# Ranks within experts: differences of router values as TensorE products, signs on VectorE and ScalarE in turn

## The chip, the cores and the metric

The kernel runs on one core of a Trainium2 chip. The metric is device time in microseconds (us) of one launch, the median of three runs. The core's engines work side by side, each through its own instructions in order: PE (TensorE, matrix products into PSUM), DVE (VectorE), ACT (ScalarE) and POOL (GpSimd); SP issues most transfers. PEld in the profile is PE's loading of stationary operands, which runs beside its products.

## What is computed

The reference is a network of four layers on 2048 tokens of 256 channels. Only the last step of the last layer is touched: a mixture of 16 experts in which each token goes to the expert with the highest router probability, and each expert takes at most 160 tokens, those with the highest probability.

```python
cap = math.ceil(CAP_FACTOR * bt / n)            # 1.25 * 2048 / 16 = 160
probs = jax.nn.softmax(jnp.einsum('btd,dn->btn', x, Wg), axis=-1)
top1_val, top1_idx = probs.max(-1).reshape(bt), probs.argmax(-1).reshape(bt)
masked = jnp.where(top1_idx[None, :] == jnp.arange(n)[:, None], top1_val[None, :], -jnp.inf)
vals, idx = jax.lax.top_k(masked, cap)          # per expert, best first
xe = x_flat[idx]
h = jax.nn.gelu(jnp.einsum('ncd,ndh->nch', xe, W1) + b1[:, None, :])
out = jnp.einsum('nch,nhd->ncd', h, W2) + b2[:, None, :]
y_flat = x_flat.at[safe_idx.reshape(-1)].set(out.reshape(-1, d), mode='drop')
```

So every token needs its rank among the tokens of its own expert: how many of them have a higher value, or the same value and a lower index. Tokens with ranks below 160 are gathered, go through two products and are written back.

## The kernel before

Tokens lie in 16 tiles of 128; four tiles make a chunk of 512. The class `Last` (from L1678) computes the ranks. Per chunk q it has three preparing steps and then one comparison ("unit") for each tile t up to the chunk's last one: 4, 8, 12 and 16 units for the four chunks, 40 in all.

- `logits` (L1739) makes the router's logits by PE, `top` (L1751) finds each token's best expert and its value by DVE, with one Exp on ACT.
- `rows` (L1771, called by `last`) turns values and experts, which lie one token per partition, into rows that lie along the free dimension and are the same on all partitions. PE transposes a broadcast (L1781), and ACT copies the result into the two halves `vb` and `eb` of `HT` (L1783). It also counts, by a product with ones (L1785), the tokens of the same expert in earlier tiles.
- `beats(t)` (L1797) compares the 128 tokens of tile t, on the partitions, with up to 512 tokens of chunk q, along the free dimension. ACT squares the difference of the experts (`l3f_dq`, L1802): zero for the same expert, at least 16 otherwise. DVE asks in one instruction whether the other value is higher and whether that 1 or 0 exceeds the square (`l3f_b`, L1822); its accumulator gives the sum along the row. PE sums the columns, 128 of them per product, against a single column of ones (`l3f_cs`, L1829), and DVE copies these sums into `acc` (L1836). Where the tile lies in the chunk itself, its own 128 x 128 square is compared apart, with ties, by three DVE instructions (`l3f_tie`, L1813, L1816, L1817).

`finish` (L1852) sends these steps out by hand: the rest of the previous mixture's additions (`c.pair`, three pairs of tiles: loads `yt<-tbuf`, DVE additions L1315, PE transposes L1241, ACT copies L1244) alternates with the steps of the four chunks. The steps of chunk 0 up to `last` are called earlier, from the loop over the shared expert (L1206). Then DVE sums `acc` into ranks (`l3f_rank`, L1875), compares them with the places 0 to 159 (`l3f_A`, L1879), PE turns that into row numbers (`l3f_pi`, L1884), and `run` (L1914) gathers rows by POOL and computes 20 slots of tokens, with results written by POOL (L1933).

Two facts of scheduling matter. Each engine takes its instructions in one fixed order, which is planned when the program is built, out of the order in which the code names them and the data they need; the planner may pull an instruction ahead of one that still waits. And tiles of PSUM are taken from pools: the tag "mm" has four buffers of one bank, "o" and "t" have two each.

Of the kernel before, what the change touches and what calls it, by code (L numbers as in the profile page):

```python
# [8 lines left out]
F32 = mybir.dt.float32  # L9
# [77 lines left out]
def _consts(k):  # L87
# [9 lines left out]
    k.after = cp.tile([P, P], F32, name="after")  # L97
    nc.gpsimd.affine_select(out=k.after, in_=k.ones, compare_op=ALU.is_ge, fill=0.0,
                            base=-1, pattern=[[-1, P]], channel_multiplier=1)
# [18 lines left out]
    k.one16 = cp.tile([P, 1], BF16, name="one16")  # L118
    nc.vector.memset(k.one16, 1.0)

# [1557 lines left out]
class Last:  # L1678

    E, F = 16, 512

    def __init__(self, k):
        self.k, E = k, self.E
        rp = k.rp
        self.w = []
        self.parts = [self.chunk(q) for q in range(NB)]

        self.plan = {5: [0], 6: [0], 7: [0]}  # L1690
        self.oh = rp.tile([P, NT, E], F32, name="l3f_oh")
        self.val = rp.tile([P, NT], F32, name="l3f_val")
        self.neg = rp.tile([P, NT], F32, name="l3f_neg")
        self.cum = rp.tile([P, NT + 1, E], F32, name="l3f_cum")

        self.acc = rp.tile([P, NT, 10], F32, name="l3f_acc")

        self.ids = rp.tile([P, NT, 2, E], BF16, name="l3f_ids")
        self.down = rp.tile([P, E], F32, name="l3f_down")
        self.th = rp.tile([P, NT], F32, name="l3f_th")  # L1700

        self.vb, self.eb = k.HT[:, 0, :], k.HT[:, 1, :]
        self.outs = []
# [11 lines left out]
    def begin(self):  # L1715

        k, nc = self.k, self.k.nc
        nc.vector.memset(self.acc, 0.0)
        nc.vector.memset(self.cum[:, 0, :], 0.0)
        nc.vector.tensor_scalar(self.down, k.iota[:, 0:self.E], -1.0, float(self.E), ALU.mult, ALU.add)  # L1720
        nc.vector.tensor_scalar_add(self.th, k.iota[:, 0:NT], 1.0)
        nc.sync.dma_start(k.hx[:, D:2 * D].rearrange("(t p) d -> p t d", p=P), k.Xt)
        self.weights()

# [4 lines left out]
    def chunk(self, q):  # L1729
# [41 lines left out]
        def rows(mul, mm):  # L1771
            nc.vector.tensor_scalar_mul(self.neg[:, ts], got["f"], -4.0)
            oh = self.oh[:, ts, :]
            nc.vector.tensor_tensor(oh, _bc(self.down, 1, [P, 4, E]), _bc(got["f"], 2, [P, 4, E]),
                                    ALU.is_equal)
            for t in range(4 * q, 4 * q + 4):
                nc.vector.tensor_add(self.cum[:, t + 1, :], self.cum[:, t, :], self.oh[:, t, :])
            for src, dst in ((got["f"], self.eb), (self.val[:, ts], self.vb)):
                ps = psum.tile([P, 4, P], F32, name="l3f_rb", tag="mm")
                for j in range(4):  # L1780
                    i = nc.tensor.transpose(ps[:, j, :], src[:, j:j + 1].to_broadcast([P, P]), k.ident)  # L1781
                    behind(i, mm)
                nc.scalar.copy(dst[:, cols], ps.rearrange("p j q -> p (j q)"))  # L1783
            ps = psum.tile([P, 4, E], F32, name="l3f_pn", tag="mm")
            i = nc.tensor.matmul(ps.rearrange("p t e -> p (t e)"), k.ones,  # L1785
                                 self.cum[:, ts, :].rearrange("p t e -> p (t e)"), start=True, stop=True)
            behind(i, mm)

            w = pool.tile([P, 4, E], F32, name="l3f_w")
            nc.vector.tensor_mul(w, ps, oh)  # L1790
            nc.vector.tensor_reduce(self.acc[:, ts, 5], w, AX.X, ALU.add)
            nc.vector.tensor_tensor(self.ids[:, ts, 0, :], oh, _bc(self.th[:, ts], 2, [P, 4, E]), ALU.mult)
            nc.vector.tensor_scalar_mul(self.ids[:, ts, 1, :], oh, k.tok[:, 0:1])

        def beats(t):

            def unit(mul, mm):  # L1797
                lo = max(t * P, q * TB)
                own = t >= 4 * q
                dq = pool.tile([P, TB], F32, name="l3f_dq", tag="fa")  # L1800
                n = (q + 1) * TB - lo
                i = nc.scalar.activation(dq[:, 0:n], self.eb[:, lo:lo + n], AF.Square,  # L1802
                                         bias=self.neg[:, t:t + 1], scale=4.0)
                v1 = self.val[:, t:t + 1]

                first = t % 4 == 0
                if first:
                    got["cs"] = psum.tile([P, 4], F32, name="l3f_cs", tag="t", bufs=2)
                a = lo
                if own:  # L1810
                    a = lo + P
                    tie = pool.tile([P, P], F32, name="l3f_tie", tag="xsT", bufs=3)
                    i = nc.vector.scalar_tensor_tensor(tie, self.vb[:, lo:a], v1, k.after, ALU.is_equal,  # L1813
                                                       ALU.mult)
                    behind(i, mul)
                    i = nc.vector.scalar_tensor_tensor(tie, self.vb[:, lo:a], v1, tie, ALU.is_gt, ALU.add)  # L1816
                    i = nc.vector.scalar_tensor_tensor(tie, tie, 1.0, dq[:, 0:P], ALU.mult, ALU.is_gt,  # L1817
                                                       accum_out=self.acc[:, t, 4:5])
                n = (q + 1) * TB - a
                if n:  # L1820
                    w = pool.tile([P, TB], BF16, name="l3f_b", tag="xs", bufs=4)
                    i = nc.vector.scalar_tensor_tensor(w[:, 0:n], self.vb[:, a:a + n], v1,  # L1822
                                                       dq[:, a - lo:a - lo + n], ALU.is_gt, ALU.is_gt,
                                                       accum_out=self.acc[:, t, q:q + 1])
                    behind(i, mul)

                    for j in range(n // P):
                        m = (a + j * P) // P - 4 * q
                        nc.tensor.matmul(got["cs"][:, m:m + 1], w[:, j * P:(j + 1) * P], k.one16,  # L1829
                                         start=first, stop=t % 4 == (2 if own else 3),  # L1830
                                         skip_group_check=True)
                        first = False
                if t % 4 == 3:

                    lo = 1 if own else 0
                    nc.vector.tensor_scalar_mul(self.acc[:, 4 * q + lo:4 * q + 4, 6 + t // 4],  # L1836
                                                got["cs"][:, lo:4], -1.0)
            return unit
# [13 lines left out]
    def finish(self, c):  # L1852
# [22 lines left out]
        nc.vector.tensor_reduce(rank, self.acc, AX.X, ALU.add)  # L1875
        ps = k.psum.tile([P, 2, 2, E], F32, name="l3f_pi", tag="t", bufs=2)
# [265 lines left out]
```

## Time and profile before

| | us |
|---|---|
| Median of 3 runs | 1601.93 (1601.33 to 1602.55) |
| The profiled execution | 1612.81 |
| Its span, first to last instruction | 1611.1 |
| First and last `l3f_tie` or `l3f_b` start | 1452.0 and 1500.3 |
| First gather of the slots (POOL L332) | 1508.84 |
| PE's mean granted clock | 0.953 of full |

Busy times in the stage (us from the span's start; from the table of stretches):

| Stretch | PE | DVE | ACT | POOL |
|---|---|---|---|---|
| 1420 to 1440 | 19.04 | 9.46 | 4.85 | 4.44 |
| 1440 to 1450 | 7.42 | 7.51 | 5.17 | 4.61 |
| 1450 to 1460 | 6.07 | 8.28 | 4.94 | 0.00 |
| 1460 to 1470 | 6.81 | 8.73 | 6.11 | 2.35 |
| 1515 to 1580 | 63.88 | 20.00 | 16.84 | 28.88 |

A time in the profile is that of one execution, which took some 11 us longer than the median. "Busy" is the time in which an engine had an instruction running. In the lines below, a group of instructions is told by its line in the code, its engine, what it writes and reads, its shape and its count, then the busy sum and the mean duration in ns, then the engine's idle time just before it and what ended that. Successive instructions on DVE and ACT overlap by some 0.07 to 0.1 us, so the step from one start to the next is shorter than the duration.

### The profile page before, as it was taken

What the parts mean: (1) busy time and instruction counts of PE and PEld (TensorE: products, weight loads), DVE (VectorE), ACT (ScalarE), POOL (GpSimd) and SP (SyncE); (2) the same over time, 40 slices, a digit from 0 to 9 for tenths busy, and PEclk for the clock granted to TensorE, in tenths of its full rate; (3) what the DMA queues carried; (4) which work ended last, traced back from release to release, by engine and by line L of the source; (5) the groups of instructions that cost most, each with busy time, mean ns of one, the idle gap of its engine ahead of it and who ended that gap; (6) DMA issues with size and microseconds to landing.
All of it is one profiled execution on the core that took longest, in us unless ns stands there. A gap on an engine that the chain in (4) does not pass through costs nothing. (4 is left out here: it accounts for less than half of the span.)

```text
span 1611.1 us, 23661 instructions
## 1 busy us (share of the span) xinstructions
PE 1466.1 (91%) x8570; PEld 1021.6 (63%) x8570; DVE 491.7 (31%) x1654; ACT 313.1 (19%) x637; POOL 293.5 (18%) x306
## 2 busy tenths in 40 slices
PE   5879998967999989999999999999999989995697
PEld 2543333533555776555599999999985448863575
DVE  3732221323411344341111111111114414459432
ACT  2312221112111212111111111111112212126322
POOL 0400000300231332023100000000000243430242
PEclk9879999977999999999999999999999999995699
DMA  9759994813211465051143255055517437573271
GB/s 241 262 181 334 343 345 161 246 54 118 83 50 40 148 210 178 27 194 49 40 172 104 101 184 169 30 181 178 175 32 259 149 118 243 186 224 124 59 242 35
DMA packets 184241, 252.46 MB, mean 157 GB/s; under 512 B 17111, under 2 KB 137823, under 8 KB 184112
## 3 DMA queue, kind: packets, MB, share of 16 engines
q1 hardware_dynamic: 164448, 210.92, 40.8%
q0 software_dynamic: 14176, 36.63, 6.4%
q10 hardware_dynamic: 5488, 3.25, 0.7%
q8 instruction: 74, 1.21, 0.3%
q14 instruction: 55, 0.45, 0.1%
HBM read 284.86 MB, written 50.76 MB: 208 GB/s over the span
## 5 line engine op out<-in xcount | busy, mean ns | idle before, releaser
L1229 PE MATMUL spo<-ring,sa 128*128 128x256 f32 x768 | 193.0, 394 | 20.9 <-DVE sa L1226 15.7
L277 POOL DMA_INDIRECT tbuf<-ys,sdst x114 | 112.2, 984 | 539.1 <-ACT ys L1432 228.4
L1229 PEld LDWEIGHTS spo<-ring,sa 128*128 128x128 f32 x768 | 140.6, 192 | 103.0 <-DVE sa L1226 71.9
L1226 DVE TENSOR_TENSOR sa<-ssg,spu 128x512 f32<-128x512 f32 x96 | 65.9, 686 | 331.6 <-PE spu L1219 284.8
L1423 PE MATMUL fpg<-xsT,ring 128*128 128x128 f32 x1152 | 141.6, 276 | 5.9 <-ACT ys L1432 5.9
L1423 PEld LDWEIGHTS fpg<-xsT,ring 128*128 128x128 f32 x1152 | 135.8, 192 | 10.4 <-ACT ys L1432 9.4
L1423 PE MATMUL fpu<-xsT,ring 128*128 128x128 f32 x1152 | 140.4, 275 | 0.0
L1423 PEld LDWEIGHTS fpu<-xsT,ring 128*128 128x128 f32 x1152 | 134.4, 192 | 0.0
L1427 DVE TENSOR_TENSOR fa<-fsg,fpu 128x512 f32<-128x512 f32 x72 | 49.5, 687 | 277.6 <-PE fpu L1423 277.6
L1430 PE MATMUL fpo<-ring,fa 128*128 128x256 f32 x576 | 130.3, 379 | 0.0
L1224 ACT ACTIVATE ssg<-spg 128x512 f32<-128x512 f32 x96 | 57.3, 597 | 349.3 <-PE spg L1219 273.1
L1430 PEld LDWEIGHTS fpo<-ring,fa 128*128 128x128 f32 x576 | 106.7, 190 | 13.0
L1219 PE MATMUL spg<-HT,ring 128*128 128x512 f32 x192 | 100.1, 609 | 5.2 <-PEq L478 2.9
L1219 PE MATMUL spg<-XT,ring 128*128 128x512 f32 x192 | 99.6, 608 | 4.7 <-ACT XT L896 4.7
L1406 PE MATMUL cpo<-ring,ch 128*128 128x256 f32 x312 | 86.8, 401 | 5.0 <-ACT ch L1403 3.5
L1219 PE MATMUL spu<-HT,ring 128*128 128x512 f32 x192 | 90.9, 594 | 0.0
L1219 PE MATMUL spu<-XT,ring 128*128 128x512 f32 x192 | 90.4, 593 | 0.0
L1400 PEld LDWEIGHTS cph<-xsT,ring 128*128 128x128 f32 x624 | 81.8, 191 | 5.0 <-ACT ch L1403 1.1
L1400 PE MATMUL cph<-xsT,ring 128*128 128x128 f32 x624 | 82.4, 275 | 0.7 <-ACT ch L1403 0.7
L1373 DVE COPY xsT<-ps_cm 128x256 f32<-128x256 f32 x138 | 56.8, 421 | 84.0 <-PE ps_cm L354 77.8
L1426 ACT ACTIVATE fsg<-fpg 128x512 f32<-128x512 f32 x72 | 43.0, 597 | 179.6 <-PE fpg L1423 179.6
L1406 PEld LDWEIGHTS cpo<-ring,ch 128*128 128x128 f32 x312 | 53.1, 189 | 19.5 <-ACT ch L1403 12.9
(550 smaller groups left out, 1606.0 us busy)
## 6 DMA issues: line engine op xcount, KB each, us to landing
ring<-in_L_w SPq DMA_DIRECT2D x108, 1024.0 KB
ring<-in_L_r SPq DMA_DIRECT2D x96, 512.0 KB
ring<-in_L_r SPq DMA_DIRECT2D x156, 256.0 KB
xs<-xbuf SPq DMA_DIRECT2D x138, 129.0 KB
ring<-in_L_W SPq DMA_DIRECT2D x32, 512.0 KB
yt<-tbuf SPq DMA_DIRECT2D x48, 256.0 KB
xbuf<-ACC SPq DMA_DIRECT2D x1, 6063.0 KB
ring<-in_L_s SPq DMA_DIRECT2D x6, 512.0 KB
```

The lines of the kernel that those rows point to most:

```text
L277: i = k.nc.gpsimd.indirect_dma_start(out=self.ap, out_offset=bass.IndirectOffsetOnAxis(ap=idx, axis=0), in_=rows, in_offset=None, **end)
L1219: mm = nc.tensor.matmul(ps, W[:, c, f * P:(f + 1) * P], X[:, c, cols], start=c == 0, stop=c == 1)
L1224: nc.scalar.activation(sg, pg, AF.Silu)
L1226: mul = nc.vector.tensor_mul(a, sg, pu)
L1229: mm = nc.tensor.matmul(po[g // 2][:, g % 2, :], a[:, g * P:(g + 1) * P], W2[:, f, :], start=f == 0 and g % 2 == 0, stop=f == nf - 1, skip ...
L1373: turned = nc.vector.tensor_copy(xT, _channel_major(k, self.psum, xs))
L1400: nc.tensor.matmul(ph[:, f, :], R1[:, c, f * P:(f + 1) * P], xT[:, c, :], start=c == 0, stop=c == 1)
L1406: nc.tensor.matmul(po, h[:, f, :], R2[:, f, :], start=f == 0, stop=f == 1)
L1423: nc.tensor.matmul(ps[:, j, :], W[:, c, (f0 + j) * P:(f0 + j + 1) * P], xT[:, c, :], start=c == 0, stop=c == 1)
L1426: nc.scalar.activation(sg, pg, AF.Silu)
L1427: nc.vector.tensor_mul(a[:, f0:f0 + 4, :], sg, pu)
L1430: nc.tensor.matmul(po, a[:, f, :], W2[:, f, :], start=f == 0, stop=f == 4 * nh - 1)
```

## The change

- `rows` no longer makes `vb` and `eb`. It builds, per token, two vectors of 128 bf16 channels in the tile `z`: the one-hot expert (16 channels, both sides), one constant channel with 1 on the left side and -1 on the right, and the value split into three bf16 parts, against 1 and -1. PE turns each side of each tile by a product with a bf16 identity (8 products per chunk), and ACT copies both sides as bf16 into the place in `HT` where `vb` was (`sides`).
- `beats(t)` computes with one bf16 product over these 128 channels, for 128 x up to 512 pairs, the difference of values, less 1 where the experts differ. It is above zero exactly where the other token is of the same expert and has a higher value. In the tile's own square a second product subtracts 1 from all pairs but those with a later index (`not16`), so that the three `l3f_tie` instructions go.
- The sign of the difference is taken by DVE for even t (2 or 0) and by ACT for odd t (Sign, 1 or -1), both out of PSUM, to bf16, with the row sum by the accumulator. The constants that make the two scales agree are put into `acc` beforehand (`begin`), and the rank is halved at the end.
- Column sums are one product per unit, with a 128 x 128 block of ones as stationary operand and up to 512 columns streamed. The sums of all units of a chunk gather in one bank; at the chunk's end ACT copies one row of it, four small f32 products turn that to the partitions, and DVE copies it into `acc`.

```diff
+    k.ident16 = cp.tile([P, P], BF16, name="ident16")
-    k.one16 = cp.tile([P, 1], BF16, name="one16")
+    k.one16 = cp.tile([P, P], BF16, name="one16")
...
-        self.acc = rp.tile([P, NT, 10], F32, name="l3f_acc")
+        self.acc = rp.tile([P, NT, 7], F32, name="l3f_acc")
...
         nc.vector.memset(self.acc, 0.0)
+        for t in range(NT):
+            c = sum((q + 1) * TB - max(t * P, q * TB) for q in range(t // 4, NB) if self.on_act(t))
+            c -= P * sum(self.on_act(u) for u in range(4 * (t // 4) + 4) if u <= t)
+            nc.gpsimd.memset(self.acc[:, t, 4:5], float(c))
+        nc.vector.memset(self.z, 0.0)
...
+    def on_act(self, t):
+        return t % 2 == 1
+    def sides(self, q):
+        x = self.k.HT[0:self.K, 0, q * TB:(q + 1) * TB].bitcast(BF16)
+        return x[:, 0:TB], x[:, TB:2 * TB]
...
         def rows(mul, mm):
-            nc.vector.tensor_scalar_mul(self.neg[:, ts], got["f"], -4.0)
...
+            nc.vector.tensor_copy(z[:, :, :, 0:E], _bc(oh, 2, [P, 4, 2, E]))
+            r = pool.tile([P, 4], F32, name="l3f_r")
+            for i in range(3):
+                to = zf[:, :, n + 2 * i + 1:n + 2 * i + self.K + 1:self.K - 1]
+                nc.vector.tensor_copy(to, _bc(v if i == 0 else r, 2, [P, 4, 2]))
+                if i < 2:
+                    nc.vector.tensor_tensor(r, v if i == 0 else r, to[:, :, 0], ALU.subtract)
+            for side, to in enumerate(self.sides(q)):
+                ps = psum.tile([P, 4, P], F32, name="l3f_ps", tag="mm")
+                for j in range(4):
+                    i = nc.tensor.matmul(ps[0:self.K, j, :], z[:, j, side, :], k.ident16, start=True,
+                                         stop=True, skip_group_check=True)
+                nc.scalar.copy(to, ps[0:self.K].rearrange("k j p -> k (j p)"))
-            for src, dst in ((got["f"], self.eb), (self.val[:, ts], self.vb)):
-                    i = nc.tensor.transpose(ps[:, j, :], src[:, j:j + 1].to_broadcast([P, P]), k.ident)
-                nc.scalar.copy(dst[:, cols], ps.rearrange("p j q -> p (j q)"))
...
             def unit(mul, mm):
-                i = nc.scalar.activation(dq[:, 0:n], self.eb[:, lo:lo + n], AF.Square,
-                                         bias=self.neg[:, t:t + 1], scale=4.0)
+                d = psum.tile([P, TB], F32, name="l3f_d", tag="mm")
+                left, right = self.sides(t // 4)[0], self.sides(q)[1]
+                i = nc.tensor.matmul(d[:, 0:n], left[:, (t % 4) * P:(t % 4 + 1) * P], right[:, TB - n:TB],
+                                     start=True, stop=not own, skip_group_check=True)
                 if own:
...
+                    nc.tensor.matmul(d[:, 0:P], k.ident16, k.not16, start=False, stop=True,
+                                     skip_group_check=True)
+                w = pool.tile([P, TB], BF16, name="l3f_b", tag="xs", bufs=4)
+                to = self.acc[:, t, q:q + 1]
+                if self.on_act(t):
+                    nc.scalar.activation(w[:, 0:n], d[:, 0:n], AF.Sign, bias=k.minus, scale=2.0 ** 30,
+                                         accum_out=to)
+                else:
+                    i = nc.vector.scalar_tensor_tensor(w[:, 0:n], d[:, 0:n], 0.0,
+                                                       k.two.to_broadcast([P, n]), ALU.is_gt, ALU.mult,
+                                                       accum_out=to)
-                    for j in range(n // P):
-                        nc.tensor.matmul(got["cs"][:, m:m + 1], w[:, j * P:(j + 1) * P], k.one16, ...)
+                if t == 0:
+                    got["cs"] = psum.tile([P, TB], F32, name="l3f_cs", tag="o", bufs=2)
+                nc.tensor.matmul(got["cs"][:, TB - n:TB], k.one16, w[:, 0:n], start=t == 0,
+                                 stop=t == 4 * q + 3, skip_group_check=True)
+                if t == 4 * q + 3:
+                    less = pool.tile([1, TB], F32, name="l3f_less", tag="fa")
+                    nc.scalar.activation(less, got["cs"][0:1, :], AF.Copy, scale=-1.0)
+                    ps = psum.tile([P, 4], F32, name="l3f_pc", tag="t", bufs=2)
+                    for j in range(4):
+                        nc.tensor.matmul(ps[:, j:j + 1], less[:, j * P:(j + 1) * P], k.ones[0:1, 0:1],
+                                         start=True, stop=True, skip_group_check=True)
+                    nc.vector.tensor_copy(self.acc[:, ts, 6], ps)
...
         nc.vector.tensor_reduce(rank, self.acc, AX.X, ALU.add)
+        nc.vector.tensor_scalar_mul(rank, rank, 0.5)
```

In `rows` the count of earlier tokens also gains a second f32 product (`k.before` with the one-hot block), and the product with the one-hot is doubled to match the scale.

## The prediction

> **What bounds the kernel now.** I looked first for where the changed lines run, then at that stretch by engine, then at the chain of waits, then at the rows that price the new work. The page's 40 slices have PE at 9 tenths nearly throughout, but at 5 and 6 in slices 37 and 38, with the clock at 5 and 6 tenths. The table of stretches (us, then busy us of PE, PEld, DVE, ACT and POOL with counts, then PE's granted clock, DMA share, GB/s) shows that place:
>
> ```profile
> core 0: us, PE busy (x) PEld busy (x) DVE busy (x) ACT busy (x) POOL busy (x), PEclk, DMA share, GB/s
> 1470.00:1475.00 5.00, 1.78 (x14) 1.50 (x12) 4.94 (x31) 3.34 (x7) 0.00 (x0) 0.50 0.19 60
> 1485.00:1490.00 5.00, 0.93 (x11) 0.60 (x11) 5.00 (x23) 3.20 (x6) 0.00 (x0) 0.50 0.00 0
> 1490.00:1495.00 5.00, 1.60 (x24) 1.11 (x24) 5.00 (x19) 4.29 (x7) 0.00 (x0) 0.50 0.00 0
> ```
>
> DVE is full, PE mostly idle and at half clock, and transfers are over. The chain of waits (start, duration, what) ends the stage with DVE's comparisons:
>
> ```profile
> 1499.98 0.27 DVE l3f_tie L1816
> 1500.35 0.31 DVE l3f_tie L1817 x2
> 1500.68 0.33 DVE l3f_rank L1875
> 1501.03 1.50 DVE l3f_A L1879
> 1502.58 4.56 PE l3f_pi L1884 x32
> ```
>
> Nothing of the slots can start before the ranks (POOL's first gather, 1508.84, waited 44.8 us for the row numbers). Weights and `hx` have landed by then. So a shift of `l3f_A` should shift the end one for one: the slots run as before.
>
> **DVE.** By steps from start to start in the timeline: 16 tie triples at 0.27 + 0.21 + 0.26 = 11.8 us; comparisons 24 x 0.67, 4 x 0.54, 4 x 0.41, 4 x 0.27 = 21.0, and 1.6 for one that took 2.31 beside POOL; ten copies of sums 0.9. Some 35 of the 46.1 busy us from 1450 to 1500 go. Added are 20 comparisons out of PSUM (16 of 512 columns, 4 of 256), priced by L1552, and in `rows` five chained small operations of 0.2 and one copy of 128 elements, 1.2 per chunk. In these groups (busy us, mean ns | idle before):
>
> ```profile
> L1822 DVE SCALAR_TENSOR_TENSOR l3f_b<-HT,l3f_val,l3f_dq 128x512 bf16<-128x512 f32 x24 | 19.1, 812 | 1.4 <-ACT l3f_dq L1802 1.3
> L1552 DVE SCALAR_TENSOR_TENSOR ACC<-spo,ACC 128x512 f32<-128x512 f32 x2 | 1.4, 692 | 1.4 <-PE spo L1229 1.4
> L422 ACT ACTIVATE HT<-ph,l_dd 128x512 f32<-128x512 f32 x8 | 5.5, 687 | 10.4 <-PE ph L420 10.4
> L770 ACT ACTIVATION_READ_ACCUMULATOR s_sm<-s_sm,s_mx 128x1 f32 x1 | 0.2, 186 | 0.0
> L1763 ACT ACT_TABLE_LOAD x1 | 1.3, 1283 | 0.0
> ```
>
> A source in PSUM costs no more than one in SBUF: 16 x 0.62 + 4 x 0.36 = 11.4, with `rows` 4.8 and small copies 0.4 it is 16.6. DVE falls to about 28 us and no longer bounds.
>
> **ACT.** 40 squares (25.8 busy) go. A Sign of 512 is priced by L422 (PSUM source, one operand per partition): 0.687 less the overlap of 0.09, plus the accumulator's read, 0.186 or, overlapped, 0.09. Between 0.69 and 0.79 I take 0.74. 12 x 0.74 + 4 x 0.63 + 4 x 0.41 = 13.0; four copies of the sums 2.0. ACT's 33 us become 22.
>
> **PE** gets the work. A unit streams its columns twice: 24 full units and, per chunk, 512 + 384 + 256 + 128 own columns, twice, plus four squares of 128: 36,864 columns. 120 narrow column sums (0.068 each, 8 us) and 32 f32 transposes (0.239 each, 7.6) go; the 32 small bf16 products in their place cost about half. No row has a wide bf16 product[...]. A recorded f32 product of 512 columns (L1219; each f32 product is recorded twice) steps 0.52 at full clock: at that price PE needs 37 us at full clock, and the gain is gone. [...]
>
> The clock is then the question. This is the restart after the ranks, now (us, PE busy, clock, DMA share, GB/s):
>
> ```profile
> 1516.00:1517.00 1.00, 1.00 (x7) 0.50 0.64 217
> 1517.00:1518.00 1.00, 1.00 (x7) 0.53 0.68 213
> 1518.00:1519.00 1.00, 0.65 (x5) 1.00 0.08 33
> ```
>
> Dense products began at 1514.16 and full clock came at about 1517.9, 3.7 us later. [...]
>
> **The sum.** Chunk 0 runs in the shadow of the additions (until 1461.2) as now. Chunk 1's values are ready at 1459.0; then five DVE steps 1.0, eight products 1.0, two copies 1.2: sides ready at 1462.3, where the first square now starts at 1461.5. From there 36 units with 33,792 columns: 17.2 warm; other PE work of the chunks (logits, transposes, counts, turned sums) 2.5; the cold 3.7 us at half rate lose 1.9; one unit's latency at the end 1.0. The last sign ends near 1484.9. ACT's share from 1462.3 is 18 and hides. The new tail is longer: last sum 0.3, copy 0.6, four f32 products 0.5, copy 0.2, sum of `acc` 0.3, halving 0.2, with hand-overs 2.3. `l3f_A` starts at 1487.2 instead of 1501.03: 13.8 saved. `l3f_pi` took 4.56 at half clock; warmer PE gives 1.0 (between 0 and 2.3). 14.8 off the profiled execution's 1612.8, and the same off the median, 1601.9: **1587**.
>
> At nothing I cost: the memsets of `begin`, since its present ones run at 391 where DVE then idles 5.5 us until `ssg` (uncovered: 2 us); constants, made in the first 4 us, while the weights come at 9.9; the deleted mask, likewise. `rows` of chunk 0 is called in the shared loop's last block, behind its last DVE product, so nobody of that loop waits for it.
>
> **Rivals.**
>
> *Lockstep: slower.* In the code's order each sum of columns follows its own sign. If PE kept that order, it would wait for each sign before the next difference: product with latency 0.4, sign 0.7, sum 0.2, hops 0.1 = 1.4 per unit, 36 units 50.4, and with 2.5 and the tail `l3f_A` is at 1517.5: **1618**. It decides when fewer than 1.5 units are in flight. The timeline speaks against:
>
> ```profile
> 1429.42 1.02 PE L1219 MATMUL spg<-XT,ring 128*128 128x512 f32 x2
> 1430.99 1.99 PE L1229 MATMUL spo<-ring,sa 128*128 128x256 f32 x8 [0.54 <-DVE sa L1226]
> 1433.04 1.02 PE L1219 MATMUL spg<-XT,ring 128*128 128x512 f32 x2
> 1433.90 1.88 PE L1219 MATMUL spu<-XT,ring 128*128 128x512 f32 x4
> 1436.63 1.99 PE L1229 MATMUL spo<-ring,sa 128*128 128x256 f32 x8 [0.41 <-DVE sa L1226]
> ```
>
> The next block's `spg` stands ahead of this block's `spo`, although the code names it after. Four "mm" banks allow four units in flight. Chance 0.06.
>
> *PE stays cold, or bf16 streams no faster than an f32 record.* [...]34.3 + 4 + 1 from 1462.3, `l3f_A` at 1503.9: **1605**, between 1597 and 1607. For it: the 32 products of `l3f_pi` kept PE busy for 4.5 us and the clock stayed at 0.50. Against: those stream 32 columns each, these 512. Chance 0.09.
>
> *Sign needs another table than Exp.* [...] The trace has one load at L1763 and then squares, copies and Exps mixed without another, but no Sign. If Sign is elsewhere, the Exps of chunks 1 to 3 cost six loads: 7.7 us by the row[...]. The row has 1.29 from load to Exp, so I take it: ACT 25 instead of 18, **1591**[...]. Chance 0.08.
>
> **Numbers.** The main case has 0.77, its own range 1578 ([...]no gaps, additions earlier by 2) to 1596 (gaps of 0.25 per unit). The range 1578 to 1600 takes in the table case and the better part of the cold one. A measurement of this kernel tells about 0.2%, 3.2 us, from no change. Faster: 0.77 + 0.08 + 0.01 = 0.86; same: 0.06; slower: lockstep 0.06 and the end of the cold case 0.02 = 0.08.
>
> **What would show it.** Right: the table of stretches shows DVE near 60% from 1462 on, PE above 85% with the clock at 1.0 after some 4 us; [...]no table load between the first and last Sign; `l3f_A` near 1487; slots unchanged from first gather to end. Wrong: the clock at 0.5 throughout, PE waiting for each sign by name, or a later first unit because `rows` is longer.

## The result and the profile after

The changed kernel takes **1595.46 us** (20 runs, 1592.38 to 1600.39), the kernel before in the same comparison 1600.36 us (20 runs, 1595.14 to 1605.51): a ratio of 0.9972, with an interval of 0.9961 to 0.9983. That is 4.9 us faster, where 14.8 were forecast. The profiled execution took 1597.45 us with a span of 1595.3.

The two profiled executions differ by 15 us, three times as much, so their spans must not be set against each other. In the two chains of waits, the last transfer of the preceding step (`tbuf`, a scatter by POOL) begins at 1422.59 in the trace of before and at 1410.97 in that of after: 11.6 us apart before any changed instruction has run. What can be compared is **the stage**, from the start of chunk 0's reciprocal (`l3f_val`, the last small step of `top`) to the start of `l3f_A`: 50.59 us before, 45.40 after, 5.2 less, which agrees with the medians. (The changed kernel, traced a second time below, has 44.44; of before there is one trace.) It splits at three instructions (start to start in the timelines, but for the end of the last comparison):

| us | Before | After | Forecast |
|---|---|---|---|
| Reciprocal of chunk 0 to that of chunk 1 | 8.44 | 9.23 | 8.44 |
| **Entry**: to the first comparison of chunk 1 | 3.39 | 8.93 | 3.4 |
| **Body**: to the end of the last comparison | 38.37 | 24.32 | 22.6 |
| **Tail**: to the start of `l3f_A` | 0.39 | 2.92 | 2.3 |
| Stage | 50.59 | 45.40 | 36.8 |

The last column is the forecast's own times (reciprocal 1459.0, sides 1462.3, last sign 1484.9, `l3f_A` 1487.2) read in the same manner, to 0.1; 0.1 is put between sides and first comparison. The table of stretches of after, in the columns of the one shown of before, has what was to be seen in the body:

```profile
core 0: us, PE busy (x) PEld busy (x) DVE busy (x) ACT busy (x) POOL busy (x), PEclk, DMA share, GB/s
1449.40:1454.40 5.00, 2.05 (x8) 1.27 (x8) 4.19 (x14) 0.74 (x2) 2.49 (x1) 0.50 0.30 105
1454.40:1459.40 5.00, 4.38 (x20) 2.64 (x21) 2.99 (x18) 2.72 (x7) 0.00 (x0) 0.52 0.44 148
1459.40:1464.40 5.00, 4.71 (x48) 3.23 (x47) 2.35 (x17) 2.90 (x9) 0.00 (x0) 1.00 0.23 67
1464.40:1469.40 5.00, 3.46 (x21) 1.65 (x22) 4.03 (x27) 1.80 (x6) 0.00 (x0) 1.00 0.00 0
1469.40:1474.40 5.00, 4.90 (x30) 2.52 (x30) 3.76 (x13) 3.89 (x11) 0.00 (x0) 1.00 0.00 0
```

DVE is no longer full, PE nearly is in most of the body (21.78 of its 24.32 us), and the clock is at 1.0 from 1459.4. Two of these rows show where time stayed: in the first, PE is busy for 2 of 5 us, and POOL for 2.49; in the fourth, PE is busy for 3.46 and DVE for 4.03.

The chain of waits at the stage's end (start, duration, what):

```profile
1481.67 0.58 PE l3f_cs L1862 x3
1482.27 0.60 ACT l3f_less L1866
1482.91 1.06 PE l3f_pc L1869 x8
1483.99 0.18 DVE l3f_acc L1871
1484.29 0.28 DVE l3f_rank L1909
1484.59 0.18 DVE l3f_rank L1910
1484.80 1.50 DVE l3f_A L1914
1486.35 4.54 PE l3f_pi L1919 x32
```

This is the new tail. Behind `l3f_A` nothing has changed: from its start to the first gather 7.81 us before and 7.78 after, from there to the start of POOL's last write of results 94.65 and 95.09.

The entry is the largest difference to the forecast. In the timeline of before (start, duration, engine, line, operation, output and inputs; in brackets the idle time before and who ended it) it is these two steps of DVE, 3.39 apart:

```profile
1458.88 0.17 DVE L1769 RECIPROCAL l3f_val<-l3f_val 128x4 f32<-128x4 f32 x1
...
1462.27 2.31 DVE L1822 SCALAR_TENSOR_TENSOR l3f_b<-HT,l3f_val,l3f_dq 128x512 bf16<-128x512 f32 x1 [0.85 <-ACT l3f_dq L1802]
```

The same stretch in the timeline of after, with DVE, PE, POOL and ACT's copies:

```profile
1448.59 1.58 PE L1869 MATMUL l3f_pc<-ones,l3f_less 1*128 1x1 f32 x8 [0.68 <-ACT l3f_less L1866]
1448.63 0.17 DVE L1798 RECIPROCAL l3f_val<-l3f_val 128x4 f32<-128x4 f32 x1
...
1450.21 0.17 DVE L1871 COPY l3f_acc<-l3f_pc 128x4 f32<-128x4 f32 x1 [1.40 <-PE l3f_pc L1869]
1450.29 0.48 DVE L1321 SCALAR_TENSOR_TENSOR ACC<-yt,l3c_g,ACC 128x256 f32<-128x256 f32 x1
...
1451.46 2.49 POOL L1876 TENSOR_TENSOR Xt<-Xt,ACC 128x1024 f32<-128x1024 f32 x1 [13.12 <-DVE ACC L1321]
...
1451.64 2.33 DVE L1812 TENSOR_TENSOR l3f_r<-l3f_val,l3f_z 128x4 f32<-128x4 f32 x1
...
1454.55 0.19 DVE L1810 CAST l3f_z<-l3f_r 128x8 bf16<-128x8 f32 x1
1454.80 1.03 PE L1816 MATMUL l3f_ps<-ident,l3f_z 128*128 128x128 bf16 x8 [2.70 <-DVE l3f_z L1810]
...
1455.50 1.07 ACT L1819 CAST HT<-l3f_ps 128x512 bf16<-128x512 f32 x2 [2.98 <-PE l3f_ps L1816]
1455.63 0.63 PE L1824 MATMUL l3f_pn<-l3f_cum,ones 128*128 128x64 f32 x2
...
1456.48 0.42 PE L1782 MATMUL l3f_pl<-ident,l3f_lt 128*128 128x128 f32 x1
1456.69 1.06 PE L1842 MATMUL l3f_d<-HT 128*128 128x512 bf16 x2
...
1457.56 0.68 DVE L1855 SCALAR_TENSOR_TENSOR l3f_b<-l3f_d,two 128x512 bf16<-128x512 f32 x1
```

Read from start to start, the 8.93 us are: 1.66 until DVE has copied chunk 0's turned sums (`l3f_pc`, which stand in DVE's queue between two small steps of chunk 1); 1.06 for the last additions and the one-hot block; 2.55 in which a subtraction of four numbers per partition (`l3f_r`) takes 2.33 us, beside POOL's addition of 2.49; 0.90 for the rest of `z`; 1.89 from PE's first product on the sides to its first difference, which needs ACT's two copies, done at 1456.57 (the counts, `l3f_pn`, and chunk 2's logits, `l3f_pl`, run on PE during these copies); and 0.87 for the first difference to reach DVE. What DVE waited for longest through the whole stage (sum, times, longest):

```profile
DVE l3f_acc L1871 <- PE l3f_pc L1869: 6.7, 4, 2.5
DVE l3f_w L1829 <- PE l3f_pn L1824: 4.4, 4, 2.0
DVE l3f_b L1855 <- PE l3f_d L1846: 2.5, 4, 0.9
```

The turned sums are waited for longest, once in each chunk.

### The profile page after: what moved, and what is told of

Its sections match the earlier page's. It is cut to its first block, busy times and chain, and to the rows that moved or that the text cites. A ratio compares the mean times of both kernels' runs of the same rounds, so it can differ in the third digit from the quotient of the medians.

```text
span 1595.3 us, 23657 instructions
## 1 busy us (share of the span) xinstructions
PE 1478.0 (93%) x8583; PEld 1024.6 (64%) x8586; DVE 475.0 (30%) x1586; ACT 303.3 (19%) x641; POOL 294.0 (18%) x321
## 3 DMA queue, kind: packets, MB, share of 16 engines
q8 instruction: 74, 1.21, 0.3%
## 5 line engine op out<-in xcount | busy, mean ns | idle before, releaser
L1412 PEld LDWEIGHTS cpo<-ring,ch 128*128 128x128 f32 x312 | 53.1, 189 | 21.2 <-ACT ch L1409 15.1
```

Of the source, the lines that this page charges most:

```text
L1412: nc.tensor.matmul(po, h[:, f, :], R2[:, f, :], start=f == 0, stop=f == 1)
```

## The experiments

Two theories. The **queue theory**: the stage's shortfall lies in what the change put into the engines' orders around the comparisons, that is in chunk 0's end (one row copied, eight product records, one copy) ahead of chunk 1's entry, and in the small subtraction that POOL's addition holds up. The **PE theory**: it lies in PE itself, in its streaming of every column twice or in its clock during the entry (a granted clock of 0.50 from 1449.0 to 1457.5 in after). All runs in one table; the ratio is to the kernel before, timed in turn with the run on the same chip, with its interval; the other columns are of the profiled execution. The medians of before were 1609.14 us beside e1, e2, e3 and e5, 1610.26 beside e6 to e9, and 1606.11 beside e0 and e10 to e12.

| Run | Entry | Body | Tail | Stage | Ratio |
|---|---|---|---|---|---|
| before | 3.39 | 38.37 | 0.39 | 50.59 | 1 |
| changed | 8.93 | 24.32 | 2.92 | 45.40 | 0.9972 (0.9961 to 0.9983) |
| e0_changed_again | 8.40 | 23.93 | 2.92 | 44.44 | 0.9970 (0.9958 to 0.9982) |
| e1_narrow_sums | 7.73 | 23.61 | 1.22 | 41.96 | 0.9926 (0.9903 to 0.9949) |
| e2_late_keep | 6.61 | 23.90 | 2.92 | 43.42 | 0.9951 (0.9934 to 0.9968) |
| e3_late_turn | 7.35 | 24.10 | 2.94 | 43.45 | 0.9953 (0.9939 to 0.9967) |
| e11_late_both | 4.78 | 23.86 | 2.95 | 40.64 | 0.9956 (0.9939 to 0.9973) |
| e6_narrow_keep | 5.56 | 23.36 | 1.22 | 39.59 | 0.9950 (0.9933 to 0.9967) |
| e12_narrow_keep_again | 5.57 | 23.32 | 1.22 | 39.48 | 0.9935 (0.9919 to 0.9951) |
| e5_all_dve | 9.22 | 29.05 | 2.95 | 50.17 | 0.9997 (0.9987 to 1.0008) |
| e8_all_dve_narrow | 8.48 | 29.66 | 1.13 | 48.27 | 0.9998 (0.9986 to 1.0010) |
| e7_counts_later | 5.98 | 25.17 | 1.21 | 40.70 | 0.9960 (0.9944 to 0.9976) |
| e9_chunk1_first | 9.60 | 24.64 | 1.22 | 42.18 | 0.9955 (0.9941 to 0.9968) |
| e10_filler | 5.53 | 25.91 | 1.22 | 43.36 | 0.9957 (0.9945 to 0.9970) |

The intervals of the ratios are 0.2 to 0.5% wide, 3 to 7 us, as wide as most steps between the runs. They tell all runs but e5 and e8 from before, and from each other only those far apart. The parts of the stage tell one mechanism from the next, each from a single trace; run again, those of the changed kernel differ by up to 0.5 and its stage by 1.0, those of e6 by 0.1. So a gain in stage against "changed" may be 1.0 smaller against e0.

### Sums of columns as before, all else changed

```diff
-                nc.tensor.matmul(got["cs"][:, TB - n:TB], k.one16, w[:, 0:n], start=t == 0, ...)
-                if t == 4 * q + 3:
-                    less = pool.tile([1, TB], F32, name="l3f_less", tag="fa")
-                    nc.scalar.activation(less, got["cs"][0:1, :], AF.Copy, scale=-1.0)
...
-                    nc.vector.tensor_copy(self.acc[:, ts, 6], ps)
+                for j in range(n // P):
+                    m = (lo + j * P) // P - 4 * q
+                    nc.tensor.matmul(got["cs"][:, m:m + 1], w[:, j * P:(j + 1) * P], k.one16[:, 0:1], ...)
+                if t % 4 == 3:
+                    nc.vector.tensor_scalar_mul(self.acc[:, ts, 6 + t // 4], got["cs"], -1.0)
```

> Undoes one part of the change: the sums of columns are again narrow products (128 columns of signs as stationary operand against one column of ones, 144 in all, four tiles into one [128, 4] block of PSUM), with ten small DVE copies; the row copy by ACT and the turned sums (4 x 8 recorded products, 1.05 us per chunk) go. Stage here means from the start of chunk 0's reciprocal to the start of l3f_A: 50.6 us before, 45.4 changed. Queue theory (the loss lies in each chunk's end, last sum - copy - turned products - copy, standing in the in-order queues of PE and DVE): 1.4 at the entry of chunk 1, some 1.0 at the end of each of chunks 1 and 2, 1.5 in the tail go, stage 40 to 42, time 4 to 5 us under the changed kernel. PE theory (PE's streamed columns bound the stage): 18,400 columns (7.7 us at full clock) are exchanged for 144 loads and narrow products of 0.05 to 0.07 (7 to 10 us), and 4.2 of turned products go: stage 41 to 45, 1 to 4 us under. If the wide sums are worth what the change puts in them: slower than the changed kernel by up to 3 us.

The stage is 3.4 us shorter than the changed kernel's: entry 1.2, body 0.7, tail 1.7, which is about what the sum lost to its row copy and its turn. 41.96 lies in what both theories expected, so this run doesn't decide between them. (The trace has 136 narrow products, not the 144 of the expectation.) It does show that the part that replaced 120 small products by 40 wide ones was a loss: the intervals of the two ratios to before, 0.9903 to 0.9949 and 0.9961 to 0.9983, don't overlap. The timeline of PE, first of after and then of this run, shows that the wide product isn't even cheaper on PE. The time of a unit's sum is from its start to the start of the next difference:

```profile
1478.23 0.38 PE L1862 MATMUL l3f_cs<-l3f_b,one 128*128 128x512 bf16 x1
1478.44 0.81 PE L1842 MATMUL l3f_d<-HT 128*128 128x512 bf16 x3
```

```profile
1483.01 0.38 PE L1842 MATMUL l3f_d<-HT 128*128 128x512 bf16 x1
1483.23 0.25 PE L1864 MATMUL l3f_cs<-one,l3f_b 128*128 128x1 bf16 x4
1483.35 0.38 PE L1842 MATMUL l3f_d<-HT 128*128 128x512 bf16 x1
```

0.21 us for 512 columns streamed, at a clock of 1.00; 0.12 for four products with the 128 x 128 blocks as stationary operand and one streamed column each. In the second fence the difference itself steps 0.22, as in after at a clock of 1.00.

### POOL's addition after the ranks

`keep` of the last chunk (POOL's `Xt<-Xt,ACC`, and the biases that are later loaded into the same place) is named after `l3f_A` and waits for it.

```diff
-            nc.gpsimd.tensor_tensor(x, x, k.Ht[:, ts, :], ALU.add)
+            i = nc.gpsimd.tensor_tensor(x, x, k.Ht[:, ts, :], ALU.add)
+            if q == NB - 1:
+                _after(k, i, [mul.ins.name])
...
-            keep(mul, mm)
+            if q < NB - 1:
+                keep(mul, mm)
...
+            made = nc.vector.tensor_tensor(A, _bc(k.iota, 1, [P, 8, CAP]), ...
...
+        self.keep_last(made, None)
```

> The changed kernel with one move: POOL's addition for the last four tiles (2.35 us, which ran from 1451.46 beside DVE's chain of chunk 1's value parts and held one of its small operations for 2.33) and its store wait for the second l3f_A, where DVE is idle. Queue theory: chunk 1's sides come 2.2 us earlier, stage 43 to 44, time 1.5 to 2.2 us under the changed kernel. PE theory: the 36 units after the entry are bound by PE's work, which begins earlier too, so also 1 to 2 under; if the entry is covered by something else (the loads of the last tiles): no change.

Entry 6.61 instead of 8.93, stage 2.0 shorter, which again both theories expected. What the run decides is who held the subtraction. In its timeline:

```profile
1459.78 0.15 DVE L1812 TENSOR_TENSOR l3f_r<-l3f_val,l3f_z 128x4 f32<-128x4 f32 x1
```

0.15 instead of 2.33, with the same instructions of DVE before and behind it. The addition's store and the loads of the biases moved too, but in after they were issued only at 1453.98 and 1455.63, when the subtraction was over. So it was POOL's addition that held it.

### The turn of the sums once, at the end

The row of each chunk stays in SBUF, and the code names all sixteen products that turn the rows in front of `l3f_rank`, with one copy by DVE.

```diff
-                    less = pool.tile([1, TB], F32, name="l3f_less", tag="fa")
+                    less = k.HT[0:1, 1, q * TB:(q + 1) * TB]
...
-                    ps = psum.tile([P, 4], F32, name="l3f_pc", tag="t", bufs=2)
...
-                    nc.vector.tensor_copy(self.acc[:, ts, 6], ps)
...
+        ps = k.psum.tile([P, NT], F32, name="l3f_pc", tag="t", bufs=2)
+        for t in range(NT):
+            nc.tensor.matmul(ps[:, t:t + 1], k.HT[0:1, 1, t * P:(t + 1) * P], k.ones[0:1, 0:1], ...)
+        nc.vector.tensor_copy(self.acc[:, :, 6], ps)
```

> The changed kernel with the turned sums put off: each chunk's row of sums is copied by ACT to a free row of HT, and the 16 small products with one DVE copy of [128, 16] stand once at the end. PE's and ACT's work is the same; DVE no longer waits for a chunk's end in the middle (1.40 before chunk 1's rows, 1.91 and 0.88 later). Queue theory: chunk 1's sides come 1.4 us earlier and the rest gains up to 1, but the tail has at worst 3 us more of small products where PE does not slip the first twelve in earlier: between 2.5 under and 1.5 over the changed kernel. PE theory: no change (within 0.5).

Entry 7.35, tail unchanged, stage 2.0 shorter (1.0 against e0), where the PE theory expected no change. In the trace PE still turns the first three chunks' rows early, at 1455.30, 1467.75 and 1479.08: the planner pulled these products forward. So what went out of the chunks' way is DVE's copy, with its wait for them.

### The two remedies together

First with narrow sums (e1 and e2 together), which makes the shortest stages of all:

> Narrow sums of columns and the late POOL addition together on the changed kernel. By the traces of the two alone the stage (start of chunk 0's reciprocal to start of l3f_A) was 41.96 and 43.42 us against 45.40. Queue theory: they are different links of one chain and add up, stage 39.5 to 40.5, ratio to the kernel before 0.992 to 0.994. PE theory: once the entry is earlier the 36 units are bound by PE and the second link hides: stage 41.5 to 42.

Then with wide sums turned late (e3 and e2 together):

> The changed kernel with wide sums kept, turned sums put off to the end, and POOL's addition late. The two alone gave stages of 43.45 and 43.42 against 45.40. Queue theory: links of one chain, they add up to 41.3 to 41.8; what it still lacks to the narrow form (39.6) is the tail, 2.9 against 1.2. PE theory (36 units bound by PE, full at full clock from the first difference on): 42.5 to 43.5.

If the causes are separate, their gains add. e1 and e2 measured 3.4 and 2.0 alone, so 40.0 was due; e6 has 39.59. e2 and e3 make 41.5; e11 has 40.64. Counted from e0 instead, 40.9 and 42.4 were due, so the gains add at least fully. Both stages lie below what the PE theory expected (41.5 to 42, 42.5 to 43.5): with e3, these are the runs that decide for the queue theory. The timeline of e6 shows the entry without both: reciprocal, additions, `l3f_r` at its ordinary price, and then the products as in after.

```profile
1455.08 0.18 DVE L1798 RECIPROCAL l3f_val<-l3f_val 128x4 f32<-128x4 f32 x1
...
1456.90 0.15 DVE L1812 TENSOR_TENSOR l3f_r<-l3f_val,l3f_z 128x4 f32<-128x4 f32 x1
...
1457.63 0.19 DVE L1810 CAST l3f_z<-l3f_r 128x8 bf16<-128x8 f32 x1
1457.88 1.03 PE L1816 MATMUL l3f_ps<-ident,l3f_z 128*128 128x128 bf16 x8 [0.52 <-DVE l3f_z L1810]
...
1460.64 0.68 DVE L1855 SCALAR_TENSOR_TENSOR l3f_b<-l3f_d,two 128x512 bf16<-128x512 f32 x1
```

From the reciprocal to PE's start it is 2.80 us instead of 6.17; from there to the first comparison 2.76 in both. So 3.4 of the entry's 5.5 us of shortfall were the end of chunk 0 and POOL's addition. What is left are the additions of the mixture and the small steps that still stand in DVE's order, and the way over PE and ACT, where the eight products of the sides take 1.03 us, as in after at a clock of 0.50. For the last word e6 was run again beside the changed kernel:

> The version with narrow sums of columns and the late POOL addition once more, beside the changed kernel on the same chip. Queue theory: stage 39.6 us again, so 5 to 6 us under the changed kernel and 10 to 11 under the kernel before, ratio 0.992 to 0.995.

> The changed kernel itself, unaltered, on the same chip as the other three of this call, for a direct comparison and a second trace. If the stage is steady from one execution to the next, it is 45.4 us again within 0.7, wherever it starts in the span; ratio to the kernel before 0.996 to 0.998.

e12 took 1594.20 us and the changed kernel 1600.53, before 1606.11. The version with narrow sums and late addition is the fastest of this comparison: by the medians 11.9 us faster than before and 6.3 faster than the change; their intervals, 0.9919 to 0.9951 and 0.9958 to 0.9982, don't overlap. Whether the late addition adds to the narrow sums, the times don't tell (e1 alone has 0.9926); only the stages do, 41.96 against 39.59 and 39.48. Two expectations missed: e6's ratio is 0.9950, not 0.992 to 0.994, and e0's stage is 1.0 shorter than the first trace's, not within 0.7.

### The signs on DVE alone

```diff
     def on_act(self, t):
-        return t % 2 == 1
+        return False
```

> The changed kernel with all 40 signs on DVE, none on ACT. DVE gets 20 comparisons more (12 of 512 columns at 0.62, the rest 0.35 to 0.5, together 10 us), ACT loses 20 Signs of 0.79 with their accumulator reads. If PE or the queues bound the stage, DVE (25 us busy of 45) has the room: within 2 us of the changed kernel. If the two sign engines bound it, the stage grows by 5 to 8 us, to 50 to 53.

> Only the first of the change's three parts: differences of values as products, but all signs on DVE and narrow sums of columns as before the change. The stage was 50.6 before, 50.17 with all signs on DVE and wide sums, 45.40 changed. If narrow sums are worth the same 3.4 us here: 46.5 to 47.5, so that differences alone bring 3 to 4 us, the split 5, and the wide sums cost 3.4. If DVE's load bounds this form (36 us busy of the stage), the narrow sums bring little: 49 to 50.

e8 is the same with narrow sums. Both stand at no change in time, 0.9997 and 0.9998, though the stage of e8 is 2.3 shorter than that of before. e5's stage grew by 4.8 to 50.17, the low end of what was expected if the two sign engines bind (50 to 53); e8's 48.27 lies between its two expectations. The differences by PE, for all the DVE and ACT work that they save, bring no measurable time by themselves here; 40 comparisons, 28 of them of 512 columns at a mean of 0.68, still go through one engine. Sharing the signs with ACT is worth 50.17 - 45.40 = 4.8 us of stage with wide sums and 48.27 - 41.96 = 6.3 (against e1) with narrow ones. That is most of what the two gain over before, 5.2 and 8.6.

### An earlier entry yet

e7 is e6 with the counts of earlier tokens moved out of `rows` to the chunk's third unit; e9 is e7 with chunk 1's preparing steps ahead of a pair of additions:

```diff
+        def counts(mul, mm):
...
+                if t == 2:
+                    counts(mul, mm)
...
-        todo = [c.pair, p0[0:2], p1[0:1], c.pair, p1[1:2], p0[2:4], c.pair, p2[0:1], p0[4:], p1[2:3], ...
+        todo = [p1[0:1], c.pair, p1[1:2], p0[0:2], p1[2:3], c.pair, p0[2:4], c.pair, p2[0:1], p0[4:], ...
```

> As the run with narrow sums and the late addition, and in addition the counts of earlier tokens (two f32 products, recorded as four, 0.85 us at half clock, which PE did between a chunk's turned sides and its first difference) are named only with the third unit of a chunk. Queue theory: 0.8 us less at the entry of chunk 1 and up to 0.5 at chunks 2 and 3 if the plan puts them behind the first differences: stage 38 to 39.5. PE theory: the same work in another order, no change against the run without it (within 0.4).

> As the run with narrow sums, late addition and later counts, with another order in finish: chunk 1's logits and top come before chunk 0's first units, and its rows before the second pair of additions. Queue theory: chunk 1's reciprocal, which came 9.2 us after chunk 0's, comes 2 to 4 us earlier and its first difference with it; what the 36 units gain depends on the data of chunks 2 and 3, which still wait for the last pairs: stage 36 to 39. If the last pairs' loads bind then, no gain: 38 to 40.

Both missed: stages of 40.70 and 42.18 against 39.59. In e7 the first comparison of chunk 1 comes 14.32 us after chunk 0's reciprocal, only 0.7 earlier than e6's 15.01. The counts had not been in the way, as its timeline shows:

```profile
1464.23 1.01 PE L1816 MATMUL l3f_ps<-ident,l3f_z 128*128 128x128 bf16 x8 [0.77 <-DVE l3f_z L1810]
1464.90 1.07 ACT L1819 CAST HT<-l3f_ps 128x512 bf16<-128x512 f32 x2 [1.03 <-PE l3f_ps L1816]
...
1466.03 1.44 PE L1845 MATMUL l3f_d<-HT 128*128 128x512 bf16 x3 [0.58 <-ACT HT L1819]
```

Without them PE waits for ACT's copies of the sides, and the first difference starts 1.80 us after PE's first product on the sides, instead of 1.89 in after.

e9 brought chunk 1's values forward, 6.72 us after chunk 0's instead of 9.45, but not its comparisons:

```profile
1458.94 0.43 DVE L1860 SCALAR_TENSOR_TENSOR l3f_b<-l3f_d,two 128x256 bf16<-128x256 f32 x1 [0.76 <-PE l3f_d L1849]
...
1464.46 0.69 DVE L1860 SCALAR_TENSOR_TENSOR l3f_b<-l3f_d,two 128x512 bf16<-128x512 f32 x1 [0.20 <-PE l3f_pl L1782]
```

The row of 256 columns is still chunk 0's third unit. Chunk 1's first, of 512, stands 16.32 us after chunk 0's reciprocal, 1.3 later than in e6: its sides were copied at 1459.11, but PE had the rest of chunk 0, chunk 2's logits and a pair's transposes ahead of the difference. So neither run has an entry that is much earlier, and what one would bring stays untested.

A regularity does show in the traces. From chunk 3's reciprocal to `l3f_A` it takes 18.16, 18.17 and 18.16 us in the changed kernel, e0 and e2, 17.5 in e3 and e11, and 15.1 to 15.5 in the runs with narrow sums (e1, e6, e12, e7, e9). Within one form, the stages differ by when chunk 3's values come: 27.25, 26.28 and 25.26 us after chunk 0's in the first three, 26.87, 24.46 and 26.63 in e1, e6 and e9. So the narrow sums earn 3.1 us behind chunk 3's values, and the late addition its share ahead of them. No run moves chunk 3's values alone, so that the end hangs on them is read from this and not shown.

### Twice the differences

Each difference product of e6 is computed twice into the same bank, the second overwriting the first, so that PE has more to do; whether its clock rises with that is what the run asks.

```diff
                 i = nc.tensor.matmul(d[:, 0:n], left[:, (t % 4) * P:(t % 4 + 1) * P], right[:, TB - n:TB],
+                                     start=True, stop=True, skip_group_check=True)
+                i = nc.tensor.matmul(d[:, 0:n], left[:, (t % 4) * P:(t % 4 + 1) * P], right[:, TB - n:TB],
                                      start=True, stop=not own, skip_group_check=True)
```

> The version with narrow sums and late addition, with each difference computed twice over (the second overwrites the first with the same values), as 40 more products for PE: 18,400 columns, 7.7 us at full clock, 15 at half. In the version without it the clock was at 0.5 in some 15 of the stage's 39.6 us. Clock theory (cold PE is what keeps the units slow): PE stays warm and the stage falls by 1 to 2 us. PE theory: PE's load is what binds, the stage grows by 3 to 8 us. Queue theory: PE has room between the waits, 39 to 41.

The table of stretches, from 20 to 30 us after chunk 0's reciprocal, first of e6 and then of this run:

```profile
1465.63:1475.63 10.00, 7.51 (x48) 5.28 (x49) 5.65 (x37) 4.11 (x10) 0.00 (x0) 0.50 0.00 1
```

```profile
1460.57:1470.57 10.00, 8.52 (x76) 5.01 (x75) 7.22 (x43) 5.23 (x14) 0.00 (x0) 0.90 0.01 2
```

The clock rose from 0.50 to 0.90, and the stage was 3.9 us longer than e12's beside it: 1.3 up to chunk 1's reciprocal, 2.6 in the body. So a warmer clock bought at that price doesn't pay, and PE's load does count: the growth is what the PE theory expected, 3 to 8. With that the PE theory holds for part of the body. The entry is the same, 5.53 beside e12's 5.57, though in e10 the eight products of the sides took 0.62 us there, as in after at a clock of 1.00, and in e12 1.04; but a difference is computed twice on that way too, so this alone doesn't clear the clock.

Leaving the sums out altogether was not tried, since the ranks address the gathers.

## Why the prediction was wrong, step by step

**The step that failed** is "Chunk 1's values are ready at 1459.0; then five DVE steps 1.0, eight products 1.0, two copies 1.2: sides ready at 1462.3", together with the line before it, "Chunk 0 runs in the shadow of the additions (until 1461.2) as now." This sum of 3.4 us to the first comparison measured 8.93. Its products and copies were priced well: 1.89 from PE's start to the first difference, where 2.2 were put. Its DVE steps were not: 6.17 from the reciprocal to PE's start, where 1.0 was put. It priced the instructions of the new `rows` and left out what stood before and among them in DVE's order: the end of chunk 0 (entry 1.2 and 1.6 shorter in e1 and e3, 0.7 and 1.0 against e0), the subtraction with two SBUF operands beside POOL's addition (2.3 shorter in e2, 1.8 against e0), and additions and other small steps, which stay in e6, where the same stretch takes 2.80. The other 0.8 us are the first difference's own way to DVE, 0.87 where 0.1 was put. The mechanism of the gain was right, its entry mis-sized by 5.5 us.

Part of this is the clock, which the forecast counted as a loss only from the first unit on. In e0, the same kernel, turning chunk 0's sums took 1.05 us, as it does in after at a clock of 1.00 (1482.91), instead of 1.58, and the entry is 8.40 instead of 8.93, shorter by just this. From PE's first product on the sides to the first difference e10, with the eight products in 0.62 instead of 1.03, has 1.62, after 1.89. So some 0.8 of the 5.5 us, an estimate from these two pairs, are half clock.

**POOL's stall was counted as removed**: "1.6 for one that took 2.31 beside POOL" was among what DVE loses. The addition stayed and held another instruction: it started at 1451.46 and took 2.49, the subtraction at 1451.64 and took 2.33. Chunk 0's one-hot block (`l3f_oh`, 128 x 64, at 1436.01) was held in the same way in after, 2.42 us beside an addition of 2.35 from 1435.99; chunk 1's took 0.22. None of the change's comparisons, which have one input in PSUM, met an addition in this trace, so what one would have cost is not shown; `rows` brought instructions that did.

**The body**: forecast 22.6, measured 24.3. PE's streaming was cheaper than forecast. The forecast's 17.2 us for 33,792 columns, 0.26 per 512, was its author's estimate, which no trace of before showed: a 512-column bf16 product steps 0.21 to 0.22 at a clock of 1.00, and the first `l3f_d` of the entry (1456.69) 0.43 at 0.50. The f32 record of L1219 doesn't step 0.52 either: in the trace of before four of them take 1.71 us from 1422.55 on, 0.43 each at a clock of 1.00, and 0.52 is a record's share of busy time (100.1 us of `spg` for 192). But a price per column was not enough: the body is not PE's stream alone. The chain of waits of after passes through the end of chunk 1 and the preparation of chunks 2 and 3:

```profile
1463.43 1.05 PE l3f_pc L1869 x8
1464.48 0.38 PE l3f_pn L1824 x2
1464.88 0.23 DVE l3f_w L1829
...
1468.57 0.15 DVE l3f_z L1810
1468.76 0.62 PE l3f_ps L1816 x8
1469.38 0.46 PE l3f_pn L1824 x4
1469.86 0.22 DVE l3f_w L1829
```

From 1463.43 to 1470.09 the chain runs over small steps, with 1.2 us of comparisons between them; chunk 1's turned sums and the counts are among them. The forecast had 2.5 for all of the chunks' other PE work and none of DVE's steps on the path. How the 1.7 us divide among these steps no run shows.

**The tail**: forecast 2.3, measured 2.92. The four f32 products are eight records of 0.13, 1.05 us, where 0.5 was put.

**The step from chunk 0's to chunk 1's values** got 0.8 longer (8.44 to 9.23, 9.19 in e0); the forecast had it unchanged, and what made it longer is not shown. So the shortfall of the stage is 5.5 + 1.7 + 0.6 + 0.8 = 8.6, and 13.8 less 8.6 is the measured 5.2.

**`l3f_pi`**: "warmer PE gives 1.0" gave nothing, 4.54 instead of 4.56. PE was at full clock until 1484 and then idle for 2.4 us, while the sums were added and `l3f_A` made. The stretches after:

```profile
1484.00:1486.00 2.00, 0.00 (x0) 0.00 (x0) 1.80 (x4) 0.15 (x1) 0.00 (x0) 1.00 0.00 0
1486.00:1488.00 2.00, 1.65 (x12) 1.23 (x12) 1.69 (x2) 0.00 (x0) 0.00 (x0) 0.62 0.00 0
1488.00:1491.00 3.00, 2.88 (x21) 2.06 (x20) 0.09 (x1) 0.00 (x0) 0.00 (x0) 0.50 0.00 0
```

**Right** were: DVE falls to some 28 busy us (28.15 in the 45.40 of the stage) and no longer bounds; the clock returns to 1.0 soon after the first units (from 1459.4); no lockstep; no table load between the first Exp and the last Sign (the next load is gelu's, at 1482.87); a shift of `l3f_A` shifts the end one for one (from `l3f_A` to the end of the span 110.1 before, 110.5 after). Sign of 512 with its accumulator's read steps 0.66 to 0.68 where two follow each other, and 0.74 was put. None of the rivals happened; lockstep's 0.4 for a product and 0.2 for a sum are near what after has, 0.38 and 0.21. Of the cold one e6 says more: a clock of 0.50 for 10 us of the body, and yet one of the two shortest stages.

**Open** stays what sets the body once the entry is short. e10 shows that more products for a warmer clock make it longer, and the reciprocals that, within one form of the sums, the end follows chunk 3's values; what would bring those earlier, no run tells. e7 and e9 were meant to shorten the entry and hardly did, so they leave it open too.

## What to carry to other kernels

Price a moved or added step together with what stands before and between its instructions in each engine's queue: here the ending of one chunk and another engine's addition made up 3.4 of the 5.5 us by which the next chunk started late. Replacing many small instructions by one wide one is a gain only if the form of its result needs no more steps; here the wide sum cost a copy, eight product records and a wait per chunk, to save instructions that were cheaper. When a full engine is relieved, look for what its relief is worth alone: moving the differences to PE gave no measurable time until a second engine took half of the signs.

## What the runs showed of the hardware

- A subtraction of 128 x 4 numbers, 0.15 us in e2 and e6, took 2.33 us in after when it met POOL's addition of 128 x 1024 (2.49): here a small instruction paid for nearly the whole of the other engine's large one. So did one with a single input: before, `l3f_neg` (128 x 4) took 2.36 beside an addition of 2.35, and 0.16 elsewhere.
- A sum of 512 columns by four products with one streamed column each steps 0.10 to 0.12 us in e1, where a 512-column difference steps 0.22, as in after at a clock of 1.00; by one product with 512 streamed columns 0.21 in after at that clock.
- f32 products with a single row and a single column cost 0.13 us per record at a clock of 1.00, two records each (after, 1482.91: four products, eight records, 1.05).
- From 20 to 30 us after chunk 0's reciprocal the narrow sums of e6 have a clock of 0.50 and the wide ones of after 1.00, and the stage is shorter nonetheless, 39.59 against 45.40: here the clock of a stage doesn't rank its versions.
- In after PE's clock fell to 0.62 (1486 to 1488) and 0.50 (1488 to 1491) after 2.4 us without a product, and 32 products of 32 columns, 4.54 us nearly without a gap, didn't bring it back.
